# A perceiver block on one core: first loads over three queues, five moved waits, and the last 65 keys over all partition quarters

## The chip, the cores and the metric

The kernel runs on one core of a Trainium2 chip. Its time is the device time in microseconds (us) of one execution; of several executions the median is given. The engines are named as in the profile: PE does matrix products (PEld is its weight loading), DVE is the vector engine, ACT the scalar engine, POOL is GpSimd, and SP does nothing but issue loads and stores. A DMA is issued by one of the queues of SP, ACT and POOL.

## What is computed

The reference, cut to what matters here (f32; 8 batches of 64 queries, 1601 keys each, width 512):

```python
x = x + xattn(layernorm(x), ctx, ctx, Wq, bq, Wk, bk, Wv, bv)
#   qp = q Wq + bq ; kp = ctx Wk + bk ; vp = ctx Wv + bv
#   softmax(qp kp^T / sqrt(512)) vp
x = x + attn(layernorm(x), ...)      # 16 heads, sigmoid instead of softmax, gates per head
x = x + ffn(layernorm(x), ...)       # each row goes to one of 8 experts
```

The change lies in the first line, apart from a few steps that were moved and one at the very end.

## The kernel before

The 512 rows of x are four tiles (p = 0 to 3) of 128 rows: two batches of 64 queries each. The keys are never projected: a tile's projected queries are multiplied with Wk transposed (`keyed`, weights `wkT`), which gives `qk`, and the scores are qk times the raw context. For that the context has to stand with its 512 features on the partitions, and that is done by DVE in 32x32 blocks.

**Context and its blocks.** For each batch of a tile three groups of 512 keys are loaded (`load_group`, L205; 1 MB each, as `cx`), and as group 3 the last 65 keys, one key to a partition, into a `tail` tile of 96 partitions whose rows 64 to 95 GpSimd clears first (L203). `turn_group` (L230) turns one group for one quarter q of the features (128 of the 512) into a block tile `T_p_q_b2`, 128 columns for each of the groups 0 to 2 and 32 columns for the tails: L232 and L239 in the profile. `blocks` makes a whole T tile out of four such transposes. There are five buffers for block tiles (`blkp`), which the tiles L of the softmax share, and twelve `slabs` of 1 MB for contexts and weights: a load waits till the slab that it gets is free.

**Scores.** `scores` (L371) does quarter q in four steps j. Each has eight small products: partition quarter a (32 features by 32 partitions of keys turned to columns) times batch b2, on separate parts of PE's array, into the four score tiles sc[a]. Their widths are

```python
    WIDTH = (416, 416, 385, 384)
```

because 65 keys on consecutive partitions fill the blocks of quarters 0 and 1 and one column of quarter 2. Each f32 product is two instructions.

**Softmax and products.** `softmax` (L384) takes the maximum of sc[0..3] on DVE, then four exponentials on ACT (L399), one for each a, each with a sum, and one for the single 65th column (L404, with a sum), and adds up the five sums and inverts them on DVE (L409, L411). `chances` (L417) transposes L group by group on PE and copies it on ACT into `pt`; `attend` (L426) multiplies pt and cx into `ac`. `divided` multiplies by the inverse sum.

**The order of the work.** PE's order is the program's throughout. In the main loop over p, the steps of tile p-1 (attention norm, `turn`, `unit_q`, `unit_k`, gates, values) and p-2 (align, sums, back, output, routing) are set between the scores and attends of tile p. `manual_schedule` fixes DVE's or ACT's order too for a stretch; elsewhere the framework's scheduler orders DVE, ACT, POOL and SP. `keep_in_program_order` pins one instruction behind what its engine was given before. At most eight loads of SP and ACT together are under way: the ninth waits for the first to land.

**The start.** SP loads x0, then wq in four parts (L83), x1 to x3, wkT in two (L88), tile 0's tails and then its six contexts. ACT issues bq and bk (L110, L111). `normal` (L256) makes the normalised rows: moments (L138, L140), the root on ACT (L261), reciprocal (L265) and product (L267); for tiles 1 to 3 all moments come first. PE projects tile 0's queries (L283), does the first half of `keyed(0)`, turns tiles 1 to 3, does the second half, and projects the others. Two `held` slabs (L898) are written by GpSimd once qpT is complete, and the contexts of tile 1 get these slabs, so they can't be loaded sooner; GpSimd's own loads (bv, lnw, ..., bo) stand behind the two copies.

**Deals.** The queries of tile p+1 are transposed on PE (`turn_queries`) and dealt out on ACT in four sets of four copies (`deal_queries`, L369) into R, one set for each partition quarter; they are spread over the attends of tile p.

**The end.** `over` (L1065) transposes the expert's hidden rows and copies them; for the last (k = 5) DVE copies one half and ACT the other (L1078). `down` multiplies (L1086), adds on DVE (L1091) and stores by an indirect DMA (L1092).

Of the kernel before, what the change touches and what calls it, by code (L numbers as in the profile page):

```python
# [17 lines left out]
P = 128  # L18
# [18 lines left out]
def perceiver_kernel(ctx: ExitStack, tc: tile.TileContext, out: bass.AP, t: dict):  # L37
# [41 lines left out]

    load_x(0)  # L80
    wq = slab("w_xWq")
    for dc in range(DC):
        nc.sync.dma_start(out=wq[:, dc, :], in_=t["xWq"][:, dc, :])  # L83
# [3 lines left out]
    for dc in (0, 2):  # L87
        nc.sync.dma_start(out=wkT[:, dc : dc + 2, :], in_=t["xWkT"][:, dc : dc + 2, :])  # L88
# [20 lines left out]

    bq, _ = load_c("xbq", [P, DC], nc.scalar)  # L110
    bk, _ = load_c("xbk", [P, DC], nc.scalar)  # L111
# [68 lines left out]
    def projected(srcT, w, name, between=None):  # L180
# [17 lines left out]
        [one.tile([96, D], F32, tag=f"tail{k}{b2}", name=f"tail{k}{b2}") for b2 in range(2)]  # L198
        for k in range(2)
    ]  # L200
    for k in range(2):
        for b2 in range(2):
            nc.gpsimd.memset(tails[k][b2][64:96, :], 0.0)  # L203

    def load_group(p, g):  # L205
        got = []
        for b2 in range(2):
            src = t["ctx"][2 * p + b2]
            if g < 3:
                c = slab(f"cx_{p}_{g}_{b2}")  # L210
                rows = src[: 12 * P, :].rearrange("(q c) d -> q c d", c=12)
                nc.sync.dma_start(out=c, in_=rows[:, 4 * g : 4 * g + 4, :])
            else:
                c = tails[p % 2][b2]
                nc.sync.dma_start(out=c[: SK - 12 * P, :], in_=src[12 * P :, :])
# [4 lines left out]
    for g in (3, 0, 1, 2):  # L220
        cxs[0, g] = load_group(0, g)
    

    NB = D // 32
    WIDTH = (416, 416, 385, 384)
# [4 lines left out]
    def turn_group(T, p, q, b2, g):  # L230
# [7 lines left out]
        else:  # L238
            nc.vector.transpose(  # L239
                T[:96, :, 384:416],  # L240
# [15 lines left out]
    def normal(tiles):  # L256
        stats = []
        for i in tiles:
# [3 lines left out]
            stats.append((mean, rs))  # L262
        xns = []
        for i, (mean, rs) in zip(tiles, stats):
            nc.vector.reciprocal(rs, rs)  # L265
            xns.append(row(f"xn{i}"))
            nc.vector.tensor_scalar(xns[-1], xs[i], mean, rs, ALU.subtract, ALU.mult)  # L267
# [116 lines left out]
    def softmax(p, sc):  # L384
# [10 lines left out]
        L = blkp.tile([P, 13, P], F32, tag="blk", name=f"L_{p}")  # L395
        sm = tiny(5, "sm", f"sm_{p}")
        for a in range(4):
            n = WIDTH[a] // 32
            nc.scalar.activation(  # L399
                L[:, :n, 32 * a : 32 * a + 32],  # L400
                sc[a][:, : 32 * n].rearrange("p (c k) -> p c k", k=32),
                AF.Exp, bias=bias, scale=scale, accum_out=sm[:, a : a + 1],
            )
        nc.scalar.activation(  # L404
            L[:, 12, 64:65], sc[2][:, 384:385], AF.Exp, bias=bias, scale=scale,
            accum_out=sm[:, 4:5],
        )
        s = tiny(1, "s", f"s_{p}")
        nc.vector.tensor_reduce(s, sm, AX.X, ALU.add)  # L409
        r = tiny(1, "r", f"r_{p}")  # L410
        nc.vector.reciprocal(r, s)  # L411
        return L, r

    def extent(g):
        return (4, P) if g < 3 else (1, SK - 12 * P)

    def chances(p, g, L):  # L417
        nch, m = extent(g)
        tp = bank4(f"pp_{p}_{g}")
        for j in range(nch):  # L420
            nc.tensor.transpose(tp[:m, j, :], L[:, 4 * g + j, :m], ident)  # L421
        pt = row4(f"pt_{p}_{g}")
        nc.scalar.copy(pt[:m, :nch, :], tp[:m, :nch, :])  # L423
        return pt

    def attend(p, g, pt, ac):  # L426
        cx = cxs.pop((p, g))
        nch, m = extent(g)
        for j in range(nch):
            for b2 in range(2):  # L430
                r = b2 * S
                rhs = cx[b2][:, j, :] if g < 3 else cx[b2][:m, :]
                nc.tensor.matmul(  # L433
                    ac[r : r + S, :], lhsT=pt[:m, j, r : r + S], rhs=rhs,
# [438 lines left out]
    def load_pair(p):  # L873
        for g in range(4):
# [23 lines left out]
    for k in range(2):  # L898
        tc.keep_in_program_order(
            nc.gpsimd.tensor_copy(slab(f"held{k}")[:, 0, 0:1], qpT[:, DC - 1, NT * P - 1 :])  # L900
        )
# [9 lines left out]
    def turn_second(g, qs=range(2)):  # L911
        for b2 in range(2):
# [7 lines left out]
    for p in range(NT):  # L920
        i = p - 2
        sc = [bank(f"sc_{p}_{a}") for a in range(4)]
        for q in range(4):
            if p == 0 and q == 0:
                nTs = [first[1, 0], first[1, 1]]
            elif p == 1 and q == 0:
                nTs = [second[1, 0], second[1, 1]]
            elif p == 0 and q == 1:
                nTs = [first[2, 0], blocks(0, 2, 1)]
            else:  # L930
                nTs = quarter(p, q + 1) if q < 3 else None
                if p == 1 and q == 1:
                    turns.__exit__(None, None, None)
# [13 lines left out]
        L, r = softmax(p, sc)  # L947
        pts = []
        if p == 0:
            turns = tc.manual_schedule(engines={mybir.EngineType.DVE})  # L950
            turns.__enter__()
# [291 lines left out]
```

## Time and profile before

| | |
|---|---|
| Runs (us) | 293.85, 294.87, 297.11; median 294.87 |
| Profiled execution | 295.13 us, span 293.4 us, mean granted PE clock 0.988 |
| Busy share | PE 95%, DVE 54%, PEld 47%, ACT 39%, POOL 20% |
| Loaded | 50.94 MB read, 197 GB/s over the span |
| Transposes of contexts on DVE (L232) | 96, 0.680 us each |
| Score products (L377) | 1024 instructions |
| Tail loads | 8 of 130 KB |

Times on a row are microseconds from the start of the span, then the duration. A line of waits reads: engine and what it was about to do, what it waited for, total us, times, longest. In a windows row the columns are the busy time of PE, PEld, DVE, ACT and POOL (with instruction counts), the granted PE clock, the share of time in which the DMA engines were busy, and GB/s. In the PEclk row of the page each digit is the clock of one fortieth of the span, in tenths, with 9 for 0.9 and more.

### The profile page before, as it was taken

The page shows a single profiled execution, that of the slowest core. Times are in us where ns is not written, and L with a number is a line of the kernel's source. Part 1 is how long each engine was busy: PE and PEld are TensorE (multiplying, and loading weights), DVE is VectorE, ACT ScalarE, POOL GpSimd, SP SyncE. Part 2 cuts the span into 40 slices and gives each one's busy share as a digit, 9 for nine tenths or more (in the row PEclk, how much of TensorE's full clock was granted, in tenths as well). Part 3 has the DMA queues.
Part 4 walks back from the last instruction along what each step waited for, and adds up shares of the span by engine and source line. Part 5 has one row for each costly group of instructions (what it writes and reads, how often), then busy time and mean ns, then how long its engine had stood idle before and what let it go on. Part 6 is the DMA issues. An engine that isn't in the chain of part 4 may idle for free. (4 is left out here: it accounts for less than half of the span.)

```text
span 293.4 us, 6408 instructions
## 1 busy us (share of the span) xinstructions
PE 277.5 (95%) x2625; PEld 136.9 (47%) x2625; DVE 159.5 (54%) x414; ACT 114.6 (39%) x239; POOL 57.5 (20%) x100
## 2 busy tenths in 40 slices
PE   5799899999899999999999999999999999999991
PEld 4666555436544334555334465434454455352320
DVE  2555285606742587956687695453371466374140
ACT  2224202864057724416975343642425434130110
POOL 4030460000360101200120310022060032413311
PEclk9999899999999999999999999999999999999997
DMA  6999980079699994000299201959991200523401
GB/s 181 359 405 391 339 343 0 1 271 407 252 329 340 357 413 145 6 3 0 84 389 367 93 4 38 369 174 340 375 378 51 74 0 2 159 91 137 154 1 46
DMA packets 20289, 57.72 MB, mean 197 GB/s; under 512 B 2274, under 2 KB 10514, under 8 KB 16544
## 3 DMA queue, kind: packets, MB, share of 16 engines
q1 hardware_dynamic: 17568, 50.37, 47.6%
q0 software_dynamic: 2400, 6.89, 6.5%
q8 instruction: 23, 0.38, 0.6%
q14 instruction: 10, 0.08, 0.1%
q10 hardware_dynamic: 288, 0.00, 0.1%
HBM read 50.94 MB, written 6.84 MB: 197 GB/s over the span
## 5 line engine op out<-in xcount | busy, mean ns | idle before, releaser
L232 DVE STREAM_TRANSPOSE T<-cx 128x512 f32<-128x512 f32 x96 | 61.8, 680 | 31.8 <-DMA cx<-in_ctx_dram 27.5
L377 PE MATMUL sc<-T,R 32*64 32x416 f32 (+2 forms) x1024 | 51.9, 515 | 2.1 <-DVE T L232 1.3
L433 PE MATMUL ac<-cx,pt 128*64 128x512 f32 x192 | 43.8, 598 | 0.2 <-ACT pt L423 0.2
L377 PEld LDWEIGHTS sc<-T,R 32*64 32x64 f32 x1024 | 28.9, 134 | 18.8 <-issue 6.8
L369 ACT COPY R<-t_rt 32x512 f32<-32x512 f32 x48 | 27.7, 577 | 0.8
L433 PEld LDWEIGHTS ac<-cx,pt 128*64 128x64 f32 x192 | 12.7, 136 | 22.4 <-issue 21.2
L1051 PE MATMUL gu<-wgu,xeT 128*32 128x512 f32 x192 | 22.9, 597 | 0.0
L509 POOL TENSOR_TENSOR gm_k<-qn_k,c_gk 128x512 f32<-128x512 f32 x4 | 5.1, 1267 | 57.3 <-DVE qn_k L504 57.3
L185 PE MATMUL p_qk<-w_xWkT,qpT 128*128 128x512 f32 x32 | 14.6, 598 | 1.6 <-DMA w_xWkT<-in_xWkT_dram 1.6
L185 PE MATMUL p_q<-w_aWq,xhT 128*128 128x512 f32 x32 | 14.8, 606 | 0.7 <-DVE xhT L480 0.7
L283 PE MATMUL qp<-xnT,w_xWq 128*128 128x128 f32 (+1 forms) x64 | 14.3, 382 | 0.5 <-ACT xnT L274 0.5
L185 PE MATMUL p_k<-w_aWk,xhT 128*128 128x512 f32 x32 | 14.7, 596 | 0.0
L185 PE MATMUL p_po<-w_xWv,acT 128*128 128x512 f32 x32 | 14.6, 592 | 0.0
L388 DVE TENSOR_REDUCE mx<-sc 128x1 f32<-128x416 f32 (+2 forms) x16 | 8.1, 566 | 11.9 <-PE sc L377 11.9
L185 PE MATMUL p_o<-w_aWo,cT 128*128 128x512 f32 x32 | 14.5, 596 | 0.0
L185 PE MATMUL p_v<-w_aWv,xvT 128*128 128x512 f32 x32 | 14.4, 592 | 0.0
L472 POOL TENSOR_TENSOR x<-x,c_bo 128x512 f32<-128x512 f32 x4 | 5.1, 1271 | 46.8 <-DVE xh L471 37.3
L423 ACT COPY pt<-pp 128x512 f32<-128x512 f32 (+1 forms) x16 | 8.0, 506 | 11.1 <-PE pp L421 11.0
L283 PEld LDWEIGHTS qp<-xnT,w_xWq 128*128 128x128 f32 x64 | 9.7, 191 | 5.2 <-ACT xnT L274 0.8
L1086 PE MATMUL y<-wd,hT 128*32 128x512 f32 x96 | 11.5, 596 | 0.6 <-DVE hT L1078 0.6
L399 ACT ACT_TABLE_LOAD x3 | 3.8, 1283 | 20.1 <-DVE bias L394 20.1
L185 PEld LDWEIGHTS p_q<-w_aWq,xhT 128*128 128x128 f32 x32 | 5.7, 189 | 9.7 <-issue 5.9
(202 smaller groups left out, 374.2 us busy)
## 6 DMA issues: line engine op xcount, KB each, us to landing
cx<-in_ctx_dram SPq DMA_DIRECT2D x24, 1024.0 KB, 8.6
wgu<-in_wgT_dram SPq DMA_DIRECT2D x8, 512.0 KB, 9.2
wgu<-in_wuT_dram SPq DMA_DIRECT2D x8, 512.0 KB, 7.8
wd<-in_wdT_dram SPq DMA_DIRECT2D x8, 512.0 KB, 7.0
rd<-blank POOLq DMA_DIRECT2D x6, 258.0 KB, 6.0
in<-rd SPq DMA_DIRECT2D x6, 258.0 KB, 3.9
xd<-blank POOLq DMA_DIRECT2D x6, 256.0 KB, 5.1
in<-xd SPq DMA_DIRECT2D x6, 256.0 KB, 7.2
```

The source lines that it names most:

```text
L185: nc.tensor.matmul(ps, lhsT=srcT[:, dc, :], rhs=w[:, dc, :], start=(dc == 0), stop=(dc == DC - 1),)
L232: nc.vector.transpose(T[:, :, 128 * g : 128 * g + 128].rearrange("p b (c k) -> p b c k", k=32), cxs[p, g][b2][:, :, 128 * q : 128 * q + 12 ...
L283: nc.tensor.matmul(ps[ec][:, : n * P], lhsT=wq[:, dc, ec * P : (ec + 1) * P], rhs=xnT[:, dc, cols], start=(dc == 0), stop=(dc == DC - 1),)
L369: nc.scalar.copy(R[32 * a : 32 * a + 32, j::4, :], tp[32 * j : 32 * j + 32, :, :])
L377: nc.tensor.matmul(sc[a][r : r + S, : WIDTH[a]], lhsT=R[32 * a : 32 * a + 32, b, r : r + S], rhs=Ts[b2][32 * a : 32 * a + 32, j, : WIDTH[a ...
L388: nc.vector.tensor_reduce(mx[:, a : a + 1], sc[a][:, : WIDTH[a]], AX.X, ALU.max)
L423: nc.scalar.copy(pt[:m, :nch, :], tp[:m, :nch, :])
L433: nc.tensor.matmul(ac[r : r + S, :], lhsT=pt[:m, j, r : r + S], rhs=rhs, start=(g == 0 and j == 0), stop=(g == 3),)
L472: nc.gpsimd.tensor_tensor(xs[i], xs[i], bo, ALU.add)
L509: nc.gpsimd.tensor_tensor(heads(gm), heads(qn), gb.unsqueeze(1).to_broadcast([P, H, HD]), ALU.mult)
L1051: nc.tensor.matmul(ps[c, :], lhsT=xTs[k][:, dc, c], rhs=ffw[e][0][:, dc, :], start=(dc == 0), stop=(dc == DC - 1),)
L1086: nc.tensor.matmul(y[c, :], lhsT=hT[:, ic, c], rhs=ffw[e][1][:, ic, :], start=(ic == 0), stop=(ic == IC - 1),)
```

## The change

It has these parts:

1. *First loads.* bq goes first on ACT's queue; wq is loaded in two parts instead of four; wkT goes to ACT's queue; the tails of tile 0 go to GpSimd's queue; bk goes to GpSimd's queue behind them.
2. *Moved waits.* The held slabs now wait for qbT (a small product that follows the projections), and GpSimd also reads wq and xnT then, so that their slabs, too, come free no sooner. Tile 1's first contexts and its tails are pinned in SP's order. Contexts are loaded in the order of groups 0, 1, tails, 2. `normal` finishes tile i-1 right after the moments of tile i.
3. *Tails.* The 65 keys are split 17, 16, 16, 16 over the four partition quarters, with a load for each; the tail tiles have 128 partitions and are cleared whole; the widths are 401, 400, 400, 400; the transposes, `chances` and `attend` of group 3 use all 128 partitions.
4. *Softmax.* The four big exponentials take 384 columns; four small ones take 17 or 16 columns, without sums, into chunk 12 of L, which DVE clears before and sums after. In tile 0 the inverse sum is worked out behind DVE's transposes for tile 1.
5. *Order in the loop.* Tile 0: the queries of tile 1 are turned behind the first transposes of L; a fifth T tile of tile 1 is begun before the last attend. Tiles 1 and 2: each of the first three deals stands one group later, behind `norm`, `logits` and, for the third, `turn`.
6. *End.* ACT copies both halves of the last hT.

```diff
+    bq = const.tile([P, DC], F32, tag="xbq", name="c_xbq")
+    nc.scalar.dma_start(out=bq, in_=t["xbq"])
     load_x(0)
     wq = slab("w_xWq")
-    for dc in range(DC):
-        nc.sync.dma_start(out=wq[:, dc, :], in_=t["xWq"][:, dc, :])
+    for dc in (0, 2):
+        nc.sync.dma_start(out=wq[:, dc : dc + 2, :], in_=t["xWq"][:, dc : dc + 2, :])
...
     for dc in (0, 2):
-        nc.sync.dma_start(out=wkT[:, dc : dc + 2, :], in_=t["xWkT"][:, dc : dc + 2, :])
+        nc.scalar.dma_start(out=wkT[:, dc : dc + 2, :], in_=t["xWkT"][:, dc : dc + 2, :])
...
-            nc.gpsimd.memset(tails[k][b2][64:96, :], 0.0)
+            nc.gpsimd.memset(tails[k][b2], 0.0)
+    REST = (17, 16, 16, 16)
+    def load_tail(p, to, src):
+        ins = (nc.gpsimd if p == 0 else nc.sync).dma_start(out=to, in_=src)
+        if p == 1:
+            tc.keep_in_program_order(ins)
...
-                nc.sync.dma_start(out=c, in_=rows[:, 4 * g : 4 * g + 4, :])
+                ins = nc.sync.dma_start(out=c, in_=rows[:, 4 * g : 4 * g + 4, :])
+                if p == 1 and g == 0:
+                    tc.keep_in_program_order(ins)
...
-                nc.sync.dma_start(out=c[: SK - 12 * P, :], in_=src[12 * P :, :])
+                k0 = 12 * P
+                for a, n in enumerate(REST):
+                    load_tail(p, c[32 * a : 32 * a + n, :], src[k0 : k0 + n, :])
+                    k0 += n
...
-    WIDTH = (416, 416, 385, 384)
+    WIDTH = tuple(384 + n for n in REST)
...
+        nc.vector.memset(L[:, 12, :], 0.0)
...
-                L[:, :n, 32 * a : 32 * a + 32],
-                sc[a][:, : 32 * n].rearrange("p (c k) -> p c k", k=32),
+                L[:, :12, 32 * a : 32 * a + 32],
+                sc[a][:, :384].rearrange("p (c k) -> p c k", k=32),
                 AF.Exp, bias=bias, scale=scale, accum_out=sm[:, a : a + 1],
             )
-        nc.scalar.activation(
-            L[:, 12, 64:65], sc[2][:, 384:385], AF.Exp, bias=bias, scale=scale,
-            accum_out=sm[:, 4:5],
-        )
+        for a, n in enumerate(REST):
+            nc.scalar.activation(
+                L[:, 12, 32 * a : 32 * a + n], sc[a][:, 384 : 384 + n],
+                AF.Exp, bias=bias, scale=scale,
+            )
+        def over_sum():
+            nc.vector.tensor_reduce(sm[:, 4:5], L[:, 12, :], AX.X, ALU.add)
...
     def load_pair(p):
-        for g in range(4):
+        for g in (0, 1, 3, 2):
             cxs[p, g] = load_group(p, g)
...
-    for k in range(2):
-        tc.keep_in_program_order(
-            nc.gpsimd.tensor_copy(slab(f"held{k}")[:, 0, 0:1], qpT[:, DC - 1, NT * P - 1 :])
-        )
+    held = [slab("held0")[:, 0, 0:1], slab("held1")[:, 0, 0:1], tiny(1, "held", "held")]
+    for to, of in ((0, qbT), (1, qbT), (2, wq[:, 0, :]), (2, xnT[:, 0, :])):
+        tc.keep_in_program_order(nc.gpsimd.tensor_copy(held[to], of[:, 0:1]))
...
+            elif p == 1 and q == 1:
+                turn_second(2, (2,), (0,))
+                nTs = [second[2, 0], blocks(1, 2, 1)]
+                turns.__exit__(None, None, None)
...
+            if p == 0 and g == 3:
+                turn_second(2, (0,), (0,))
+                second[2, 0] = block_tile(1, 2, 0)
+                for gg in (0, 3, 1):
+                    turn_second(gg, (2,), (0,))
             if p > 0 and g == 3:
                 do((turn, p - 1))
+            if 0 < p < NT - 1 and g > 0:
+                deal_queries(R, turned_qk, g - 1)
...
             attend(p, g, pts[g], ac)
-            if p < NT - 1 and g < 3:
+            if p == 0 and g < 3:
                 deal_queries(R, turned_qk, g)
...
-            for ic, copy in enumerate((nc.vector.tensor_copy, nc.scalar.copy)):
+            for ic in range(IC):
...
-                copy(hT[:, ic, :], tp[:, 0, :])
+                nc.scalar.copy(hT[:, ic, :], tp[:, 0, :])
```

## The prediction

> **What bounds the kernel now.** I read the page first, then the waits of the matmul engine (PE), then its timeline, then one-microsecond windows of the start and of 29 to 38 us.
>
> ```profile
> span 293.4 us, 6408 instructions
> ...
> PE 277.5 (95%) x2625; PEld 136.9 (47%) x2625; DVE 159.5 (54%) x414; ACT 114.6 (39%) x239; POOL 57.5 (20%) x100
> ...
> PEclk9999899999999999999999999999999999999997
> ```
>
> PE is busy for 95% of the span, so only three things can shorten it: PE's waits, PE's own work, and the slice (29 to 37 us) in which its clock is an 8. The waits of PE between 0 and 150 us:
>
> ```profile
> PE p_qk L185 <- DMA w_xWkT<-in_xWkT_dram: 1.6, 1, 1.6
> PE sc L377 <- DVE T L232: 1.3, 1, 1.3
> PE sc L377 <- DVE T L239: 0.9, 1, 0.9
> PE p_q L185 <- DVE xhT L480: 0.7, 1, 0.7
> PE pl L716 <- ACT shares L708: 0.6, 1, 0.6
> ```
>
> PE's timeline around the first scores, and in a stage without stalls:
>
> ```profile
> 17.50 10.48 PE L283 MATMUL qp<-xnT,w_xWq 128*128 128x384 f32 x32
> ...
> 30.67 0.91 PE L377 MATMUL sc<-T,R 32*64 32x416 f32 x2
> 32.84 4.71 PE L377 MATMUL sc<-T,R 32*64 32x416 f32 x62 [1.26 <-DVE T L232]
> 37.48 0.33 PE L331 MATMUL t_qb<-ident,qbT 128*128 128x128 f32 x1
> ...
> 115.03 3.02 PE L377 MATMUL sc<-T,R 32*64 32x416 f32 x64
> 117.98 0.66 PE L177 MATMUL t_q<-ident,qn_q 128*128 128x128 f32 x4
> ```
>
> A quarter of scores (64 instructions) takes 2.95 us at 115 us. The first one begins at 30.67, stops after one product, and ends at 37.48. The windows say why (columns: PE, PEld, DVE, ACT, POOL busy, PE clock, DMA share, GB/s):
>
> ```profile
> 29.00:30.00 1.00, 1.00 (x19) 0.83 (x21) 1.00 (x2) 1.00 (x4) 1.00 (x2) 1.00 1.02 217
> 32.00:33.00 1.00, 0.16 (x8) 0.16 (x16) 0.93 (x2) 0.00 (x0) 0.85 (x2) 1.00 0.97 354
> 34.00:35.00 1.00, 1.00 (x24) 0.80 (x16) 0.00 (x0) 0.00 (x0) 0.00 (x0) 0.50 1.00 397
> ```
>
> It waits for the last context tile to land and be turned, and then runs at half clock for 3.4 us (33.87 to 37.28). This place costs about 3.9 us against 2.95, the largest single loss.
>
> **Part 1, first loads and moved waits.** *When PE could start the scores.* The first product with wkT waits till 12.68; its other input, qpT, is ready at 11.60. wkT now travels beside wq, so it should no longer be last. x0 lands 0.3 later (estimate: its packets alternate with wkT's), so this product starts near 11.8. But x1 to x3, down at 9.60, now come behind 3.15 MB instead of 2.1: at the 385 GB/s of 8 to 9 us up to 2.7 us later, 0 if the start is faster; I take x1 at 10.4. DVE's work for three tiles is 3x(0.69+0.18)+3x(0.13+0.55) = 4.6, so the last xn comes at 15.0 (14.04 before). One transposition (0.44) and half of keyed(0) (1.72) follow: projection at 17.2 instead of 17.50. Gain 0.3, bounds -1.3 and +0.65. Scores could start at 30.4.
>
> *When the last T is ready.* Before: 32.73. Context landings are 2.48 apart (18.24, 20.73, ... 28.19); the last was due at 30.67 and came at 32.08, 1.4 late. In those windows the rate fell to 266 and 217 GB/s, while tile 1's tails (issued at 15.48) and, from 28.9, GpSimd's seven small loads ran. The new waits put all of these behind qbT (about 31.0): -1.4 (bounds 0, -1.4). At the start DMA moved only 1.19 MB from 2 to 7 us (198 to 303 GB/s, 420 later); at 420 that is 2.8 us, so at most 2.2 to win. [...] I take 0.9, because SP's queue was held up (x's second and third and wkT issued only at 3.15 to 6.1) and wq's rows double to 4 KB. [...] T ready: 32.73-1.4-0.9+0.5 = 30.9.
>
> *Then* the quarter runs from 30.95 in 2.85 us, to 33.8 instead of 37.48: **3.7**. Is the half clock gone too? [...] The row shows 0.50 in just the window after this wait, full before and after: I go by the row.
>
> *Cover.* Eight tail loads on GpSimd at the 0.54 of its loads take 4.3 us from about 3.5; behind them are bk (wanted at 29.66) and the query copies at 18.35. They land near 16 to 19 if the 8 to 11 us to landing of its later loads holds; DVE turns them first, then waits for contexts from 18 anyway. Tile 1's loads go out at 31.2 instead of 28.05: four contexts at 2.5 and the tails land by 44 to 46, wanted from 45.7 and 48.1 (49.48 less 3.7, plus four transposes). A microsecond lost there is still covered by DVE's 8.7 us wait for the third context group. GpSimd's bias loads land near 40; the first user is at 51. For tiles 1 to 3 SP issues 8 tail loads instead of 2, +6x0.4 = 2.4 us; contexts queued behind wait for slabs far longer (52.8 us in all on PE). If one came without cover, 2.4.
>
> **Part 2, widths.** The widest of four concurrent products falls from 416 to 401. 64 instructions are 8 rounds of 8; 2.95/8 = 0.369 a round. Two 128x512 passes 0.43 apart are 0.84 ns a column: 416 make 0.349, plus 0.02. So 15 columns are 0.0125 a round, 0.1 a quarter, 1.6 over 16 quarters if nothing else limits. In tile 0 DVE needs 6.1 us from the end of quarter 0 for three T tiles and quarters 1 and 2 now need 5.7+0.3: only quarter 3 gains, **0.1**. Tiles 2 and 3: T is ready at 126.7 and PE wants it at 126.95, so of 0.4 I take 0.25 each: **0.5** (0 to 0.8). Tails on 128 partitions change nothing: transposes, copies and products go by columns (POOL's memset is 0.52 for 32 and for 128 partitions).
>
> **Part 3, softmax.** ACT loses a one-column exponential with its read (0.27+0.22) and gets four of 16 or 17 columns: about +0.6 a tile. PE's transposes of the first groups need the four big ones only. In tile 0 turning the queries later removes waits of 0.23 and 0.24, the 0.6 eats most: **0.1** (-0.25 to 0.25). In tiles 1 to 3 ACT idles 2.03, 1.23 and 0.84 just before pt: 0, and 0.6 each if that were gone. DVE gains a memset and a 128-column sum (0.25, between the 0.16 and 0.55 of its reductions), in waits of 2.51, 2.04 and 0.71: 0; without that cover 0.35 each.
>
> **Part 4, tile 1's T order.** Before, DVE does three and a half T tiles from 69.69 to 78.85, and PE waits 0.88. Most of T(1,2,0) now lies in DVE's wait before 68.4 (1.6 us). Then 69.69+1.3+0.65 = 71.65; the next needs a block slot that frees at quarter 0's end, 71.9; three tiles at 1.97 end at 77.85. Quarter 3 starts at 77.9, not 78.91, and is 0.1 shorter: **1.1** (0.5 to 1.3).
>
> **Part 5, deals and end.** Tile 2: shares is copied at 144.68 because four deal copies (2.34) stand ahead; behind them no longer, so the 0.55 goes: **0.5** (0 to 0.55). The sigmoid then waits for them, as does DVE's "by", some 1.8 us; T tiles are wanted 15 us later. The last query deals end after unit_q as before (112.4, wanted at 115.03). The 0.65 at 104.53 is DVE's order, untouched: 0 (to 0.65). At the end hT's first half waits for DVE's y addition (284.35 to 285.0), though PE's transposes were done near 284.5; ACT alone copies both in 2x0.27 and y starts near 284.95, not 285.29: **0.3**.
>
> **Sum:** 3.7+0.1+0.5+0.1+1.1+0.5+0.3 = 6.3. The profiled execution took 295.13 (span 293.4 and 1.73 around it): **288.8**. The median of the runs shown, 294.87, is 0.26 lower, so 2.1% faster than the median.
>
> **Rivals.** [...] (b) *x1 to x3 come late and PE runs thin from 12 to 17 us*: projection at 18.5, and half clock falls on it (1.7). Scores at 33.4, end 36.2: gain 1.3+2.6 = 3.9, 291.2. Against it: 1.59 us idle at 11.09 left the clock at 1.00. (c) *The narrower widths do nothing*, because their sum is 1601 as before: without Part 2 and the shorter quarters, -0.8, 289.6. Against it: short score-like products (al, 64 columns) follow each other in 0.016, so issue isn't the limit. (d) **Slower:** GpSimd's tail loads starve beside two full hardware queues. DVE must turn tails first, and has 5x0.2+15x0.65 = 10.8 us of T work behind them. Up to a landing at 20 nothing is lost. Each later microsecond moves the scores by one and brings back the half clock: quarter 0 ends at landing+10.8+2.85+1.7. It cancels the other 2.6 when it ends at 40.1, so from a landing at 24.7 the kernel is slower; at 28 by 3.3, 298.4. Against it: GpSimd's loads of 28.9 to 32.3 landed in at most 11.0.
>
> **How the numbers follow.** Mine 0.50 (own range 286.5 to 290.6), (a) 0.20, (b) 0.12, (c) 0.08, (d) 0.10. Under 291.9 is faster by 1%, about what a measurement of this kernel can tell: all of mine and (c), 0.10 of (b), 0.11 of (a): 0.79. Slower 0.08 from (d), the rest, 0.13, within 1%. The range, 286.0 to 292.8, takes in (a), (b), (c) and my bounds and leaves out (d) and the edges.
>
> **What would show it.** wkT's wait gone; the row of 30.67 going on without the 1.26; no 0.50 window near 34; quarters at 2.85; no wait on T L239 over 0.4 near 75; no wait for shares; y after ACT's copies. I am wrong if PE waits for T past 32, if xn arrives after 16, if a tail's landing stops DVE after 20, or if a half-clock window appears at another place.

## The result and the profile after

The changed kernel takes 291.44 us (median of 20 runs, 290.71 to 294.07), the kernel before took 294.18 in the same session (20 runs, 291.96 to 297.99). The ratio is 0.9922 [0.9902, 0.9943]: 0.8% faster, where 2.1% was forecast. (Ratios, here and below, leave out executions over 1.5% longer than the fastest of the same kernel; the medians do not.) The profiled execution took 291.26 (span 289.4), against 295.13 (span 293.4).

The page of the changed kernel, its first lines and the clock row:

```profile
span 289.4 us, 6479 instructions
...
PE 276.2 (95%) x2625; PEld 132.6 (46%) x2625; DVE 160.7 (56%) x421; ACT 116.5 (40%) x248; POOL 62.6 (22%) x111
...
PEclk9999999999999999999999999999999999999998
```

The 8 in the clock row at 29 to 37 us has gone. PE still is busy for 95% of the span, so its waits are again what to read. Waits of PE up to 150 us in the changed kernel (total, times, longest):

```profile
PE qp L301 <- DMA w_xWq<-in_xWq_dram: 1.5, 1, 1.5
PE t_xn L177 <- DVE rs_a L274: 0.9, 1, 0.9
PE t_xn L177 <- DVE xn L276: 0.5, 1, 0.5
PE al L561 <- DVE kT L547: 0.4, 1, 0.4
PE sc L395 <- DVE T L252: 0.2, 1, 0.2
```

The waits for wkT (1.6), for the last T (1.3), for xhT (0.7) and for the shares (0.6) have gone, and the one on tile 1's T fell from 0.9 to 0.2. Two waits at the start are new, for wq and for tile 3's moments (rs_a). PE's timeline in the changed kernel, at the start and at the first scores (start, duration, instruction, and in brackets the idle time ahead of it):

```profile
8.23 6.51 PE L301 MATMUL qp<-xnT,w_xWq 128*128 128x128 f32 x32 [1.52 <-DMA w_xWq<-in_xWq_dram]
...
20.64 10.48 PE L301 MATMUL qp<-xnT,w_xWq 128*128 128x384 f32 x32
...
33.81 2.94 PE L395 MATMUL sc<-T,R 32*64 32x401 f32 x64
36.69 0.33 PE L349 MATMUL t_qb<-ident,qbT 128*128 128x128 f32 x1
```

The projection of tile 0 starts 0.98 later than before and takes 6.51 us where it took 3.84; that of tiles 1 to 3 starts at 20.64 instead of 17.50; the scores start at 33.81 instead of 30.67. From there nothing stalls: quarter 0 takes 2.88 us to its end at 36.69, 0.79 earlier than before. DVE's timeline shows what the projection of tiles 1 to 3 had to wait for (rows between left out):

```profile
13.58 0.69 DVE L138 BATCH_NORM_STATS2 st_a<-x 128x6 f32<-128x512 f32 x1 [8.04 <-DMA x<-in_x_dram]
...
15.46 0.16 DVE L274 RECIPROCAL rs_a<-rs_a 128x1 f32<-128x1 f32 x1 [0.18 <-ACT rs_a L281]
```

x1 can be read at 13.58, not at 9.60, though SP had issued all three x loads between 2.20 and 4.19. A second input comes late almost to the same moment: the square roots (rs_a) stand behind the copies of tile 0's qpT on ACT, and these behind tile 0's projection, which had waited for wq. The first of them is ready 0.18 after DVE's moments. So about 3 us of what the moved waits and the earlier contexts gave back were spent at the start. At its last products with wd (y) the kernel is 4.19 ahead (281.10 against 285.29): 0.79 gained up to the end of quarter 0, and 3.40 behind it.

### The profile page after: what moved, and what is told of

Same layout as the page of the kernel before. It is cut to its first block, busy times and chain, and to the rows that moved or that the text cites. A ratio compares the mean times of both kernels' runs of the same rounds, so it can differ in the third digit from the quotient of the medians.

```text
span 289.4 us, 6479 instructions
## 1 busy us (share of the span) xinstructions
PE 276.2 (95%) x2625; PEld 132.6 (46%) x2625; DVE 160.7 (56%) x421; ACT 116.5 (40%) x248; POOL 62.6 (22%) x111
## 5 line engine op out<-in xcount | busy, mean ns | idle before, releaser
L395 PE MATMUL sc<-T,R 32*64 32x400 f32 (+1 forms) x1024 | 48.0, 500 | 0.2 <-DVE T L252 0.2
L395 PEld LDWEIGHTS sc<-T,R 32*64 32x64 f32 x1024 | 22.2, 131 | 20.4 <-issue 15.7
L301 PE MATMUL qp<-xnT,w_xWq 128*128 128x128 f32 (+1 forms) x64 | 17.0, 438 | 1.5 <-DMA w_xWq<-in_xWq_dram 1.5
L301 PEld LDWEIGHTS qp<-xnT,w_xWq 128*128 128x128 f32 x64 | 12.3, 244 | 6.5 <-ACT xnT L292 1.9
L406 DVE TENSOR_REDUCE mx<-sc 128x1 f32<-128x400 f32 (+1 forms) x16 | 8.1, 568 | 9.1 <-PE sc L395 9.1
L1091 DVE TENSOR_TENSOR h<-gu,h 128x256 f32<-128x256 f32 x6 | 2.6, 425 | 14.1 <-ACT h L1090 14.1
```

Of the source, the lines that this page charges most:

```text
L301: nc.tensor.matmul(ps[ec][:, : n * P], lhsT=wq[:, dc, ec * P : (ec + 1) * P], rhs=xnT[:, dc, cols], start=(dc == 0), stop=(dc == DC - 1),)
L395: nc.tensor.matmul(sc[a][r : r + S, : WIDTH[a]], lhsT=R[32 * a : 32 * a + 32, b, r : r + S], rhs=Ts[b2][32 * a : 32 * a + 32, j, : WIDTH[a ...
L406: nc.vector.tensor_reduce(mx[:, a : a + 1], sc[a][:, : WIDTH[a]], AX.X, ALU.max)
```

## The experiments

Each is compared with the kernel before on the same chip. One of them was the kernel before itself; it came out at 0.9955 [0.9921, 0.9989] of its own time, so half a per cent is not to be told from nothing here.

**wkT back on SP's queue.** Theory A was that wkT on a second queue takes turns from wq and x1 to x3; B, that GpSimd's tail loads do; C, that the half clock sets the start.

```diff
-        nc.scalar.dma_start(out=wkT[:, dc : dc + 2, :], in_=t["xWkT"][:, dc : dc + 2, :])
+        nc.sync.dma_start(out=wkT[:, dc : dc + 2, :], in_=t["xWkT"][:, dc : dc + 2, :])
```

> The changed kernel with one edit undone: wkT's two loads go to SP's queue again, behind x1 to x3. Theory A (wkT's second queue takes every second packet turn from wq and from x1 to x3, and that is what made PE start the scores 3.1 us late): the first wait of the projection for wq (1.5 us) goes, x1 is down near 10 instead of 13.6, the projection of tiles 1 to 3 starts near 17.5 instead of 20.6, the scores near 30.7, and the span falls by 2.5 to 3, to 286.5 to 287. Theory B (the tails on GpSimd's queue hold up x1 to x3): x1 stays at 12.5 or later, the span moves less than 0.8. Theory C (the half clock in the first projection is what is lost, and it falls where it falls): the first projection still takes 6.5 us in some executions, span within 1 of 289.4.

Measured: 289.16, ratio 0.9839 [0.9754, 0.9924]. PE's timeline of this kernel:

```profile
7.36 4.84 PE L301 MATMUL qp<-xnT,w_xWq 128*128 128x128 f32 x32 [0.46 <-ACT xnT L292]
12.26 1.95 PE L185 MATMUL p_qk<-w_xWkT,qpT 128*128 128x512 f32 x4
14.05 0.60 PE L177 MATMUL t_xn<-ident,xn 128*128 128x128 f32 x4
15.26 1.28 PE L177 MATMUL t_xn<-ident,xn 128*128 128x128 f32 x8 [0.61 <-DVE rs_a L274]
```

The wait for wq has gone, x1 is read at 7.88 (13.58 in the changed kernel), the projection of tiles 1 to 3 starts at 18.10, the scores at 31.27, and quarter 0 ends at 34.15 instead of 36.69: moving one load back is worth 2.5 us there. The whole time shows less: the profiled execution has a span of 288.6 where 286.5 to 287 was expected, and is only 0.83 ahead of the changed kernel at the last y, with waits of 1.1 for xhT (none there) and 1.2 for kT (0.9). Four executions do not settle the rest. What the second queue did is seen in the packets of the changed kernel, counted in its trace by their start: at 7 to 9 us, 96 packets of 4 KB of SP's queue and 95 of ACT's went through; from 5 to 7 us only 48 and 68, which took 180 and 283 ns in the median, against 159 from 7 to 9. So wq and the x loads behind it got half the turns or less, and for two microseconds there were fewer turns as well. Windows of both kernels say the latter once more (last column GB/s), first the changed kernel, then this one:

```profile
5.00:6.00 1.00, 0.52 (x3) 0.41 (x3) 0.54 (x1) 0.00 (x0) 1.00 (x2) 1.00 0.92 213
6.00:7.00 1.00, 0.71 (x4) 0.30 (x2) 0.00 (x0) 0.26 (x1) 1.00 (x3) 1.00 0.90 262
```

```profile
5.00:6.00 1.00, 0.32 (x2) 0.22 (x2) 0.69 (x2) 0.00 (x0) 1.00 (x3) 1.00 1.04 422
6.00:7.00 1.00, 0.90 (x4) 0.49 (x3) 0.00 (x0) 0.07 (x1) 1.00 (x3) 1.00 0.98 375
```

The same low rates stand in other kernels with wkT on ACT's queue, and not in those with wkT and the two-part wq on SP's (list at the end). A wait is left at 15.26: with the changed order of x's moments DVE does tile 3's (0.87) between xn1 and xn2, though x3 has landed.

**wkT on ACT's queue alone**, in the kernel before (one line, as above, the other way round).

> The kernel before with one edit of the change: wkT's two loads on ACT's queue. Theory A: x1 lands at 12 or later instead of 9.6, the projection of tiles 1 to 3 starts 1.5 to 3 later than 17.50, although wkT's own wait (1.59) goes; since T is ready only at 32.7, the span rises by 0 to 1.5. If the second queue shortens the start (as the prediction had it, gain 0.3): projection at 17.2 or earlier, span down by up to 0.3.

Measured: 292.5, ratio 0.9955 [0.9926, 0.9983]. The start shows the same damage in the other kernel: x1 read at 11.82 (9.60), projection at 18.87 (17.50), scores at 32.04 (30.67). The last context is turned from 31.73, 0.35 earlier than before; as the scores start 1.37 later, quarter 0 takes 3.40 without a half-clock window, and ends at 35.44. For the start, A holds from both sides. For the time it missed: 0 to 1.5 more was expected, and the median is 1.0 below that of the kernel before, 0.45% by the ratio.

**Tile 0's tails on SP's queue**, in the changed kernel.

```diff
-        ins = (nc.gpsimd if p == 0 else nc.sync).dma_start(out=to, in_=src)
+        ins = nc.sync.dma_start(out=to, in_=src)
```

> The changed kernel with one edit undone: tile 0's eight tail loads go to SP's queue, behind x1 to x3 and ahead of the contexts. Theory A: x1 still lands at 13 or later, less at most 0.7 for the 260 KB of tails that no longer share; the projection of tiles 1 to 3 starts at 20 or later, span 289 to 290. Theory B: x1 is down by 10.5, the projection starts by 18, span near 287.

Measured: 290.73, ratio 0.9893 [0.9811, 0.9975]. The wait for wq (1.28), the slow projection of tile 0 (6.71) and the projection of tiles 1 to 3 at 20.63 all stay. But x1 is read 2.1 earlier, against theory A, which had it at 13 or later:

```profile
11.46 0.70 DVE L138 BATCH_NORM_STATS2 st_a<-x 128x6 f32<-128x512 f32 x1 [5.86 <-DMA x<-in_x_dram]
...
15.45 0.16 DVE L274 RECIPROCAL rs_a<-rs_a 128x1 f32<-128x1 f32 x1 [2.16 <-ACT rs_a L281]
```

So B is half right. GpSimd's loads do hold up x1: from 9 to 11 us the core moves 402 and 395 GB/s here, 311 and 248 in the changed kernel, and SP's packets of 2 KB take 84 ns in the median instead of 132. For PE this is worth nothing, because DVE then waits 2.16 for the square root on ACT, behind tile 0's projection, which is late for wq. Both inputs have to come earlier; taking wkT off the second queue does that.

**More idle turns**, in the changed kernel, to tell the clock from the loads.

```diff
-    idle_turns(14)
+    idle_turns(16)
...
         turn_x(0, normal([0])[0])
+        idle_turns(6)
```

> The changed kernel with PE kept busy at the start: 16 idle transpositions ahead of x0's instead of 14, and 6 more while it waits for wq. Clock theory: full clock comes at about 7 us instead of 13.66, and the projection of tile 0 takes 3.84 to 4.2 us instead of 6.51 and ends near 12.2 instead of 14.74. What then sets the projection of tiles 1 to 3 tells the share of clock and loads: if loads bound it (x1 is down only at 13.58, and DVE needs some 4.6 us from there), the projection starts at 19.9 to 20.4 instead of 20.64 and the time gains at most 0.7; if the clock bound it, the projection starts at 18 to 18.5 and the time gains 2 or more.

Measured: 291.33, ratio 0.9947 [0.9913, 0.9982]. PE's timeline:

```profile
8.53 2.02 PE L301 MATMUL qp<-xnT,w_xWq 128*128 128x128 f32 x16 [1.51 <-DMA w_xWq<-in_xWq_dram]
12.28 2.02 PE L301 MATMUL qp<-xnT,w_xWq 128*128 128x128 f32 x16 [1.72 <-DMA w_xWq<-in_xWq_dram]
...
20.42 10.48 PE L301 MATMUL qp<-xnT,w_xWq 128*128 128x384 f32 x32
```

The first projection now runs at full clock (16 products in 2.02; 32 took 3.84 in the kernel before), and then stands until 12.28 for wq's second half; tiles 1 to 3 start 0.22 earlier. Of the 3.1 us lost the clock alone holds 0.2: with tile 0's projection out of the way, DVE goes on without a wait from x1 at 13.71. The loads bound the start; C is a companion, not the cause.

**The moved waits alone**, in the kernel before (GpSimd's late loads held on qbT, wq and xnT; tile 1's first loads kept in order; groups loaded in the order 0, 1, 3, 2).

```diff
-    for k in range(2):
-        tc.keep_in_program_order(
-            nc.gpsimd.tensor_copy(slab(f"held{k}")[:, 0, 0:1], qpT[:, DC - 1, NT * P - 1 :])
-        )
+    held = [slab("held0")[:, 0, 0:1], slab("held1")[:, 0, 0:1], tiny(1, "held", "held")]
+    for to, of in ((0, qbT), (1, qbT), (2, wq[:, 0, :]), (2, xnT[:, 0, :])):
+        tc.keep_in_program_order(nc.gpsimd.tensor_copy(held[to], of[:, 0:1]))
```

> The kernel before with only the moved waits: held slabs on qbT, wq and xnT kept, tile 1's first contexts and its tails pinned, groups loaded as 0, 1, tails, 2. If the late last context (32.08 instead of 30.67) came from tile 1's loads and GpSimd's small ones: it lands by 30.8, PE's wait of 1.26 shrinks below 0.3, no half-clock window near 34, the first quarter of scores ends near 34 instead of 37.48, span 290 or less. If it came from the six contexts themselves: landing at 31.7 or later, wait and half clock stay, span 293 to 294.

Measured: 292.2, ratio 0.9968 [0.9942, 0.9993]. The profiled execution, the fastest of its 20 (290.47), turns the last context from 30.11 instead of 32.08, the wait of 1.26 and the half-clock window are gone, and quarter 0 runs from 30.29 to 33.82. That is the 3.7 of the prediction, nearly to the tenth (37.48 less 33.82), but in one execution and by other terms: the first loads are those of the kernel before here, and the scores start 0.38 earlier all the same. The medians are only 1.3 apart (293.46 over 39 runs of the kernel before); where the other executions lose the rest was not seen.

**The moved waits undone**, in the changed kernel (the same hunk, reversed).

> The changed kernel with GpSimd's held-back loads waiting for qpT as in the kernel before (the moved waits undone, all else as changed). Theory (the moved waits are what lets the last context land early; they made it land 2 us earlier when tried alone): the late loads run at 26 to 33 us beside the last contexts and tile 1's, the last T comes at 32 to 33 again; but the scores start only at 33.8 in the changed kernel, so little of it reaches PE: quarter 0 ends 0 to 0.5 us later than 36.69, and the time is 0 to 0.6 above the changed kernel's 291.44. Rival (the waits still carry the gain of the changed kernel): a wait of over 1 us on the last T and a half-clock window behind it come back, and the time is 1.5 to 2.5 above.

Measured: 292.55, ratio 0.9995 [0.9958, 1.0031]. In the profile the last T is in time without them (turned from 30.35, quarter 0 ends at 36.22, even earlier than 36.69): the loads wait for qpT, and qpT itself is 3 us late here. So in this execution nothing is lost at this place without the waits; the late start does their work. The median is 1.1 above the changed kernel's, in another session, where 0 to 0.6 was expected; the profile places 0.6 of that (a wait of 0.32 for xhT, and 0.25 more for kT), the rest stays open.

**The old order of x's moments**, on top of wkT on SP's queue: `normal` as it stood in the kernel before.

> This is the run with wkT back behind x1 to x3 on SP's queue, and the moments of tiles 1 to 3 taken all ahead of the first reciprocal again, as in the kernel before. Theory (the changed order costs time once x1 to x3 land early: DVE did tile 3's 0.69+0.18 us of moments between xn1 and xn2, although x3 had long landed): the third xn comes at 14.9 instead of 15.8, PE's wait of 0.61 for it falls under 0.1, the projection of tiles 1 to 3 starts near 17.3 instead of 18.10, and the median is about 0.8 us under that run's 289.16. Rival (ACT's order sets it: the square roots stand behind the four copies of qpT): the reciprocal starts at 12.9 in both, the projection moves by less than 0.3, and so does the time.

Measured: 288.78, ratio 0.9862 [0.9802, 0.9922]. The wait of 0.61 went as expected (PE does all twelve transpositions from 15.09 on without a stop). But this execution stood 2.67 for wkT, so the projection came at 18.12 all the same. The step on DVE is shown, its worth in time is not.

**Square roots first**, on top of that: `normal` is cut in two, so that the square roots of tiles 1 to 3 stand ahead of the copies of qpT in ACT's order.

```diff
-        turn_x(0, normal([0])[0])
+        turn_x(0, finished(*moments_of([0]))[0])
+        rest = moments_of(range(1, NT))
         project_q(0, 1, [bank(f"qp0_{ec}") for ec in range(DC)])
-        later = normal(range(1, NT))
+        later = finished(*rest)
```

> The run with wkT back on SP's queue and the old order of moments, and in addition the square roots of tiles 1 to 3 ahead of the copies of qpT in ACT's order. Theory (ACT's order holds the reciprocal at 12.92 although x1 is down at 7.9): the first reciprocal comes near 9, the three xn are ready by 12.5, PE goes through the transpositions without a wait, the projection of tiles 1 to 3 starts at 16.5 to 17.0 instead of 18.10, and the median is 287.8 to 288.3, 1 us or so below 289.16. Rival (the copies between the transpositions and the half clock on tile 0's projection set it): projection at 17.3 or later and the time no lower than with the old order alone.

Measured: 289.14, ratio 0.9874 [0.9823, 0.9925]. The xn are ready at 13.0, projection at 17.17, scores at 30.34, quarter 0 ends at 33.64: 0.5 ahead of the run with the old order, as far as the start goes. In this execution the lead is gone again further on, with a wait of 0.32 for xhT and 0.36 more for kT, and the median is no lower.

**The rest alone**: the kernel before with all but the first loads, the moments' order and the moved waits.

> The kernel before with everything of the change but the first loads, the order of x's moments and the moved waits (so: shared-out keys, widths, softmax, order of tile 1's turns, deals, end; tile 0's tails stay on SP's queue). Theory (these parts gave 3.2 of the 4.2 us, independent of the start): scores start at 30.7 and quarter 0 ends near 37.4 as before; from there the milestones run ahead of the kernel before by 0.7 at the first attention, 2 at the end of tile 1's scores, 2.6 to 3.3 from tile 2 on; the span is 290.2 to 290.8, the ratio to the kernel before 0.989 to 0.991. Rival (they gain only because the later start gave the turns and loads more lead): the wait on T near 75 to 79 stays at 0.5 or more, and the span is 291.5 or longer.

Measured: 292.94, ratio 1.0017 [0.9982, 1.0053]. The theory fell for the time: quarter 0 ends at 36.24, but the projection starts at 18.99, and tile 0's takes 6.29 where the kernel before took 3.84. From the end of quarter 0 to the last y it takes 245.73 us, where the kernel before took 247.81 and the changed kernel 244.41. The parts behind quarter 0 do gain; something ahead of it takes that back in the other executions.

**The first loads as before**, all else changed, names it.

> The changed kernel with the first loads of the kernel before (all on SP, wq in four, wkT behind x1 to x3, tile 0's tails on SP, old order of moments), but with the moved waits and all later parts. Theory (the split of the first loads over queues costs the start some 2 to 3 us, the moved waits take away the late T, the rest gives 2.4 to 3.4 from the end of quarter 0 on): projection of tiles 1 to 3 at 17.1 to 18.2, quarter 0 ends at 33.8 to 34.8 instead of 36.69, and the median is 288.0 to 289.5, ratio to before 0.980 to 0.988. Rival (tile 0's eight tails on SP's queue in place of two push the contexts back, which is why the rest alone came out no faster): the last T is late again, quarter 0 ends at 36 or later, and the time is no better than the changed kernel's 291.44.

Measured: 293.05, ratio 0.9995 [0.9959, 1.003]. The rival is right about what happens, though the reason is not the issuing. SP's timeline in this kernel, its DMA issues:

```profile
4.61 1.98 SPq L89 DMA_DIRECT2D w_xWkT<-in_xWkT_dram  x2
6.70 7.94 SPq L209 DMA_DIRECT2D tail<-in_ctx_dram  x8
14.69 3.18 SPq L220 DMA_DIRECT2D cx<-in_ctx_dram  x6
```

and what PE makes of it:

```profile
31.74 0.85 PE L390 MATMUL sc<-T,R 32*64 32x401 f32 x2 [0.64 <-DVE T L245]
34.11 4.52 PE L390 MATMUL sc<-T,R 32*64 32x401 f32 x62 [1.52 <-DVE T L245]
```

Shared out to four partition quarters, the last keys need eight loads, and SP is at them for 7.94 us. A row of the timeline takes in the waits between its issues, so the issues themselves (durations in ns) and SP's waits up to 20 us have to be read too:

```profile
L209 SPq DMA_DIRECT2D tail<-in_ctx_dram x8: 230/310/320, 6.7 to 14.3; - x8
```

```profile
SPq L209 <- DMA w_xWkT<-in_xWkT_dram: 2.6, 2, 1.6
SPq L209 <- DMA w_xWq<-in_xWq_dram: 1.6, 2, 1.2
SPq L209 <- DMA x<-in_x_dram: 1.1, 3, 0.4
```

An issue takes 0.31; 5.3 of the 7.94 SP waits for wq, x and wkT to land, because at most eight loads of SP and ACT are under way and every tail takes a place. (In the kernel before and in the changed one never more than eight were under way; in the first, the ninth, x2, waited 0.3 for bq to land and went out at 3.85.) The contexts go out at 14.69, after wkT has landed, where the kernel before sent them at 8.84 and the changed kernel at 4.24. The last context is turned from 33.35 (30.11 with the moved waits alone), PE waits twice (0.64 and 1.52), and the rest of its quarter takes 4.52, much like the 4.71 of the kernel before, where the clock was 0.50 for 3.41 of them. So with an early start tile 0's tails are better on GpSimd's queue, outside the eight (SP sent the first context at 4.24 while GpSimd was issuing them, from 3.2 to 7.1, in the changed kernel). The nearest kernel that has them there, the one with the old moments on top of wkT on SP's queue, turns the last context from 29.86 and ends quarter 0 at 34.16; it differs in the parts of wq and in bq and bk as well, so the tails' queue alone was not tried. Of SP's 7.94 us the issue time is the small part (8 x 0.31); the larger one is the waiting for a place (5.3).

**The kernel before, profiled again.**

> The kernel before, unchanged, profiled a second time. The prediction took the stall of the first execution's profile (last T 1.26 us late, then 3.4 us of half clock; quarter 0 ends at 37.48, span 293.4) as what every execution has. Theory (it is one of several courses: other executions of it take 290.6 to 292.5, below that one's 295.1): this execution has a shorter wait or no half-clock window behind it, quarter 0 ends between 33.5 and 36, and the span is 289 to 291.5. Rival (the stall is in every execution, and the scatter comes from later): quarter 0 ends at 37 to 37.6 again and the span differs elsewhere.

Measured: 293.44; the profiled execution 293.52. PE's timeline:

```profile
29.77 0.91 PE L377 MATMUL sc<-T,R 32*64 32x416 f32 x2
32.34 4.71 PE L377 MATMUL sc<-T,R 32*64 32x416 f32 x62 [1.67 <-DVE T L232]
36.98 0.33 PE L331 MATMUL t_qb<-ident,qbT 128*128 128x128 f32 x1
```

The theory fell: the late T and the slow quarter are there again, in an execution at the median. The wait of 0.65 for xhT is not. So both profiled executions of the kernel before have the stall that the prediction took away, and the failure isn't to be blamed on an odd profile.

**Widest product 416 again**, in the changed kernel, with the same sum of columns.

```diff
-    REST = (17, 16, 16, 16)
+    REST = (32, 11, 11, 11)
```

> The changed kernel with the last 65 keys split 32, 11, 11, 11 instead of 17, 16, 16, 16: the same sum of columns, 1601, but the widest of the four concurrent products is 416 again. Prediction's Part 2 (the widest of the four sets a round, 0.84 ns a column): a quarter of scores takes 2.95 to 3.02 instead of 2.88 to 2.94 us, and the kernel 0.5 to 1.0 us more than the changed one. Rival (c) of the prediction (the sum sets it): quarters as in the changed kernel within 0.02 us, and the same time.

Measured: 292.39, ratio 0.9969 [0.9942, 0.9995], 0.95 above the changed kernel's median, in another session. Two lines of PE's timeline give the quarter:

```profile
33.41 3.01 PE L395 MATMUL sc<-T,R 32*64 32x416 f32 x64
36.35 0.33 PE L349 MATMUL t_qb<-ident,qbT 128*128 128x128 f32 x1
```

2.94 from the first product to what follows, 2.88 in the changed kernel, 2.95 at 115 us in the kernel before. The widest of the four counts, and not only the sum: rival (c) of the prediction falls. The price is not the prediction's 0.1 in each quarter. It is 0.06 or 0.07 in the first quarters of tiles 0, 2 and 3, 0.01 to 0.03 in the last two of tiles 2 and 3, and in tile 1 the second and third quarter take 5.71 together against 5.39. PE is busy with scores for 49.2 us in all, against 48.0 in the changed kernel. Part of these 1.2 can be T tiles that came late; the prediction let part of the quarters count and came to 0.6.

**Copies on ACT**: xhT and kT written by ACT alone, on top of the square roots first.

```diff
-        nc.vector.tensor_copy(kT, transposed(kn, f"k{i}"))
+        nc.scalar.copy(kT, transposed(kn, f"k{i}"))
```

> The run with wkT on SP's queue and the square roots first, and in addition the copies xhT and kT on ACT alone, so that they no longer stand behind the turns of T in DVE's order. Theory (the waits for xhT, 0 to 1.1 us by when tile 2's context lands, and for kT, 0.3 to 0.7 in tile 2 and 0.5 in tile 3, come from the turns queued ahead on DVE): all three waits go, the span is 285.9 to 286.5, the median 0.8 to 1.4 below the run without it. Rival (ACT's own queue, with the copies of R and a table load of 1.28 ahead, is as late): a wait of 0.3 or more on ACT takes their place and the time doesn't change.

Measured: 287.15 (286.55 to 288.12), ratio 0.9814 [0.9781, 0.9847]; 2.0 below the run without them (another session), where 0.8 to 1.4 was expected. What PE waits for in this kernel, after its two longest waits, which lie at the start:

```profile
...
PE t_c L177 <- DVE cg L594: 0.7, 1, 0.7
PE qp L299 <- ACT xnT L290: 0.5, 1, 0.5
PE p_qk L185 <- ACT qpT L304: 0.4, 1, 0.4
PE y L1109 <- ACT hT L1101: 0.3, 1, 0.3
PE sc L394 <- DVE T L252: 0.2, 1, 0.2
```

All waits for xhT and kT are gone, and nothing on ACT takes their place: the waits for ACT in the list lie at the start and at the end. The wait for cg has grown from 0.4 to 0.7. This version beats both: by 1.9% the kernel before; its median is 4.3 us below the changed kernel's, in another session. **The same two copies with the first loads as before:**

> The same with the copies xhT and kT on ACT alone. Theory: the waits for xhT and kT go as they did in the run with the square roots first (3 waits, 1.5 us there); 1.0 to 1.6 below the kernel with the old first loads, 286.6 to 288. Rival (the waits were gone or hidden with this start): the same time within 0.4.

Measured: 291.13, ratio 0.991 [0.9866, 0.9953]; 1.9 below the kernel without them, with the T wait of 1.52 and the slow quarter (4.63 behind the wait) still there. The theory's level (286.6 to 288) fell with that of the old first loads, the gain from the copies stands, measured here in one session, and is above the 1.0 to 1.6 expected.

## Why the prediction was wrong

The direction was right and the sum too large. It gave 6.3: 3.7 for Part 1 and 2.6 for the others. In the profiles Part 1 gave 0.8 and the others 3.4.

- **The step that failed** is "When PE could start the scores": x1 at 10.4, projection at 17.2, scores at 30.4. Measured: 13.58, 20.64, 33.81. Two terms of it were wrong. (A third, x0 later by 0.3 because its packets alternate with wkT's, was wrong too but decided nothing: x0 is read at 3.52, 0.18 earlier than before, and wkT's first packet starts at 3.37.) The delay of x1 to x3 behind wkT was bounded by 2.7 us at a steady 385 GB/s, and then taken as 0.8. With wkT on the second queue alone it was 1.9 to 2.2 (x1 at 11.46 with the tails on SP's queue, 11.82 in the kernel before with wkT moved), within the bound; GpSimd's eight tail loads made it 4.0, and their effect on the x loads stood in no term. And the delay of wq was put at nothing: it shared its turns with wkT (96 and 95 packets from 7 to 9 us), PE stood 1.52 for it, tile 0's projection was slow (6.51 us instead of 3.84, with full clock recorded only from 13.66), and ACT's square roots for tiles 1 to 3 came behind that. In the profile the two end 0.18 us apart, so taking away one of them gives little (0.01 with the tails on SP's queue, though x1 is 2.1 earlier there). Moving wkT back took both away and gave 2.5 us at the end of quarter 0 (theory A, from both sides).
- **When the last T is ready** was nearly right: 30.9 forecast; in the changed kernel the last contexts are turned from 30.52, the first of them is done at about 31.2 (0.65 a transpose), and PE doesn't wait. The half clock behind it is gone too, as the trace's row said. But the reason was only half right. The moved waits do it in the kernel before; in the profile of the changed kernel without them the last T is in time as well, since qpT came late. No run shows the +0.5 that its sum has for the shared-out tail rows; what the runs show in its place is where the tails' loads stand, and what they take from the others. What was missed is the places: eight tails take eight of the loads under way, where the prediction priced only their issues (0.4 each, for tiles 1 to 3; 0.31 was measured). On SP's queue, with the first loads otherwise as before, they make quarter 0 end at 38.6, later than in the kernel before. What rival (d) feared did not come: GpSimd's tails were issued from 3.2 to 7.1 and took 6.6 to 7.6 to land, the last by 13.8, where 16 to 19 was forecast, and DVE never waited for them. It was they that slowed the other queues (311 and 248 GB/s from 9 to 11 us, 402 and 395 with the tails on SP's).
- **Rival (b)**, x1 to x3 late and the half clock on the projection, came nearest: scores at 33.4 and 291.2 in all were forecast for it, at a chance of 0.12; 33.81 and 291.44 were measured. That its numbers fit so well is partly luck. It had the projection of tiles 1 to 3 at 18.5 and the half clock on that one; it came at 20.64 and ran at full clock (10.48 as before), and the half clock fell on tile 0's. The objection to it, that 1.59 us idle had left the clock alone, was drawn from a PE already at full clock (from 6.57 in the kernel before). In the changed one full clock came at 13.66, 7.09 us later, after a wait of 1.52 for wq. (These are the traces' first records of the clock; ahead of them the windows print 1.00 whatever it was, as tile 0's projection shows with 6.51 against 3.84.)
- **The others**, from the milestones. Widths: quarter 0 takes 2.88 (2.85 forecast), tile 0's other three 8.93 (9.02 before); tile 2 and 3 gained, and gave it back in new waits of 0.40 and 0.54 for kT, which stands behind the turns on DVE. Softmax and the later query turns in tile 0: 0.57 (0.1). Tile 1: 1.3 (1.1), its quarters' widths among it. Shares: 0.70 (0.5). End: 0.44 (0.3). The wait for xhT, costed at nothing, went with 0.65 to 0.70. It can't be credited to the change: the copy stands behind turns of tile 2's context, and by its landing the wait was 0.65 and 0 in two executions of the kernel before, 0 to 1.1 in the experiments. Without it the others gave 2.7. That tails on 128 partitions change next to nothing held: a transpose took 0.27 us on 96 partitions and on 128 (medians of 266 and 273 ns), a copy 0.26 and 0.27 and a product 0.61 and 0.61 on 65 and on 128.

Against its own execution the kernel gained 3.9 instead of 6.3. The 2.4 between them are 2.9 missing in Part 1, less 0.8 more in the others, and 0.3 behind the last y. Not settled: why the moved waits alone keep less in the median than in their profile, and the last 0.5 of what their undoing costs.

## What to carry to other kernels

At the start of a kernel the order in which bytes are wanted is the order to keep: a load that is wanted third, put on a second hardware queue, took every second packet from the first two here (96 and 95 packets in 2 us). Where the number of loads under way is limited, as to eight here, each small load takes a place as a big one does; GpSimd's queue spared these places here, but its loads slowed what was moved beside them (311 and 248 GB/s against 402 and 395). Before a row of merged issues is read as a cost of issuing, the waits in it have to be taken out. And a stall that is taken away shows its worth only as far as the next thing that is late: work out when every input of the next stage arrives, and price the delayed ones at the end of their bound, not at the kind end.

## What the runs showed of the hardware

- SP's and ACT's queues of 4 KB packets were served about one for one (96 and 95 in 2 us). While they began, from 5 to 7 us, the core moved 213 and 262 GB/s (221 and 274 with the tails on SP's queue, 150 and 240 in the kernel before with wkT moved). With wkT on SP's queue and wq in two parts it was 422 and 375 (389 and 377 with the old moments, 401 and 383 with the square roots first). One queue is not enough for that: the kernel before, with wq in four parts of 2 KB rows, moved 215 and 303. Why is open.
- GpSimd's eight tail loads slowed the other queues while they ran: 311 and 248 GB/s from 9 to 11 us, SP's packets of 2 KB at 132 ns in the median, against 402 and 395 GB/s and 84 ns without them. Why is open.
- An issue of a tail of 16 or 17 rows on SP took 0.31 us (0.23 to 0.32 for tile 0's eight), one of 65 rows in the kernel before 0.31 to 0.42.
- PE's speed at the start went with fractions of a microsecond. Of eleven executions that did not wait for wq, four of the five with at most 0.52 us idle ahead of x0's transpositions did the first projection in 3.84, one in 5.54; the six with 0.68 to 0.92 took 4.8 to 6.3.
- Later, the length of a wait alone did not decide: waits of 1.59 (kernel before) and 2.67 (old moments) for wkT were followed by no slow stage (the projection of tiles 1 to 3 took 10.48 behind both), waits of 1.26 and 1.67 in the scores by a rest of the quarter of 4.71 (at a clock of 0.50 for 3.41 us in the first execution).
